# The first tokens of layer 2 summed during the last blocks of layer 1, and layer 1's last blocks in the opposite order of experts

## The chip, the core and the metric

The kernel runs on one core of a Trainium2 chip. The metric is the device time of one execution in microseconds (us), as a median of several runs. TensorE (PE) multiplies and transposes, VectorE (DVE) and ScalarE (ACT) work on elements, GpSimd (POOL) issues the gathers and scatters here, and SyncE (SP) issues nearly all other transfers.

## What is computed

A graph network of four layers on N = 2708 tokens of D = 256 features, with a dense adjacency matrix `adj`. The layer concerned is layer 1's feed-forward part and the start of layer 2's attention:

```python
def _L1_ffn_ref(x, W1, b1, Wg, bg, Wd, bd):
    H = gelu(x @ W1 + b1)                     # 256 -> 1024
    probs = softmax(H @ Wg + bg)              # 8 experts
    assign = argmax(probs)                    # one expert for each token
    for e in range(8):
        y = H @ Wd[e] + bd[e]                 # 1024 -> 256
        out = out + where(assign == e, probs[:, e:e+1] * y, 0.0)
    return out
...
x = x + L1_gnn(layernorm(x), adj, ...)
x = x + L1_ffn(layernorm(x), ...)
x = x + L2_gnn(layernorm(x), adj, ...)        # h = x @ W.T, attention over adj
```

## The kernel before

**Tiles.** Tokens lie in 22 tiles of 128 (the last has 20). `x` stays on chip with the features along a row. Layer 1 takes the tiles in three groups, 0 to 7, 8 to 15 and 16 to 21 (`GROUPS1`).

**Sending tokens to experts.** For each group, `send1` makes H (1024 wide), writes its rows to `hid` in DRAM (`keep`, two times four DMAs for each pair of tiles), finds each token's expert, and lets `route` (L385) work out each token's place in a list sorted by expert. `scatter` (L510, issued at L513 on POOL) writes (token, probability) there, to `taken`. So an expert's tokens form stretches of the list, which `blocks` (L423) cuts into blocks of 128 rows, with the expert of each block (`ei`) and the rows to be read (`ix`). The first nine blocks (`NA`, called full) are cut from the first two groups, so that they can be worked on while the third is still sent; the other fifteen (`ALWAYS`, called rest here) follow, and are taken in the order that `in_thirds` (L1066) gives. If tokens are spread more unevenly, more than fifteen are needed: `count_left` finds how many are left over, `blocks_left` loads that into a register of each engine (for block 13), and `run_rest` (L632) has a branch, `tc.If(left > 0)` in L634, behind the last block, in which up to six more run.

**A block** (class `Units`, L638) takes these steps. POOL gathers its 128 names (`fetch_names`, L657 by L527), then the 128 rows of H for them, 512 KB (`fetch_rows`, L667). SP loads the expert's matrix, 1152 KB, into one of three buffers (`weights1`, L1070, the DMA at L1077); that DMA is made only if the buffer holds another expert's matrix. PE transposes the rows (`turn`, eight of L678), ACT copies them (L679). PE multiplies, 16 matmuls in L729. DVE adds the bias (L730) and scales by the probability (L731), and POOL scatters the rows to `given` in DRAM (L513). `more` (L689) keeps names, rows and matrices fetched ahead, the matrices two blocks. `pieces` (L709) is a generator: `send1` calls `next(fill)` to put steps of the full blocks between steps of the third group.

**Order.** The program's scheduler keeps the order of the text unless `after`, `engine_after`, `in_order` or `behind` add dependencies. [...] POOL issues names, rows and scatters of all blocks in one sequence, and SP the writes of `hid`, the matrices and the loads of layer 2.

**Layer 2's front.** `turned_up` (L1428) takes two or four tiles (`FOURS`: one group of 2, then five of 4). SP loads their rows of `given` (buffer `mine`, by `load_tiles`, L56), DVE or POOL adds them to x (L1441; DVE for tiles 0 to 5, POOL for the rest), PE transposes (L1446), ACT copies (L1448), DVE makes the norm's statistics (L193). `valued` (L1452) multiplies by the layer's matrix (L267), ACT and DVE make `hh` and `sc` (L1461, L1464), `row_scores` (L1362) turns the scores. Each load waits for all scatters to `given`, and for the branch. Then the attention's long loop runs (L1540 on DVE, L1548 on PE).

Of the kernel before, what the change touches and what calls it, by code (L numbers as in the profile page):

```python
# [15 lines left out]
P = 128  # L16
N = 2708
# [49 lines left out]
def adj_ffn4(ctx: ExitStack, tc: tile.TileContext, a: dict, out: bass.AP):  # L67
# [355 lines left out]
    def blocks(pool, brief, known, NB, B, name, done=None, full=False, least=0):  # L423
# [26 lines left out]
        if done is not None:  # L450
            rest = pool.tile([P, E], F32, name="b_rest")
            v.scalar_tensor_tensor(rest, done, -float(B), cnt, op0=ALU.mult, op1=ALU.add)
            if least:
# [9 lines left out]
        bi = count[:, :NB, None]  # L463
        v.tensor_tensor(hot, bi.to_broadcast([P, NB, E]),
                        end[:, None, :].to_broadcast([P, NB, E]), ALU.is_ge)
# [3 lines left out]
        v.tensor_scalar(ei, eb[:, :, 0], float(E - 1), None, op0=ALU.min)  # L469
        v.tensor_tensor(vec[:, 0, :], nb[:, :, 0], end, ALU.subtract)  # L470
# [35 lines left out]
        return ei, ix, end[:, E - 1 :], nb[:, :, 0]  # L506
# [131 lines left out]
    class Units(Blocks):  # L638
# [3 lines left out]
        def __init__(self, pool, given, weights, hidden):  # L642
# [3 lines left out]
            self.names = pool.tile([P, MOST, 2], F32, name="names")  # L646
            g.memset(self.names, 1.0)
            self.hs = [pool.tile([P, HC * P], F32, name="hs", tag="hs", bufs=3) for _ in range(3)]
            for h in self.hs:
                g.memset(h, 0.0)  # L650
# [12 lines left out]
        def fetch_rows(self):  # L663
# [5 lines left out]
                                 bounds_check=n - 1, oob_is_err=False)  # L669
            self.got = i.ins.name  # L670
            self.rows.append((m, h))

        def turn(self, pool, h):
            hT = pool.tile([P, HC, P], F32, name="hTs", bufs=2)
# [7 lines left out]
        def begin(self, items):  # L682

            self.names_todo = list(items)
            self.todo = list(items)
            self.rows_todo = len(items)
            self.more(False)

        def more(self, weights=True):  # L689
            while self.names_todo and len(self.named) + len(self.rows) < len(self.hs) + 1:  # L690
                self.fetch_names(self.names_todo.pop(0))
            while self.rows_todo and len(self.rows) < len(self.hs):
                self.fetch_rows()
                self.rows_todo -= 1
            while weights and self.todo and len(self.ahead) < 2:
                self.fetch(self.todo.pop(0))

        def add(self, items):
            self.names_todo += items
            self.todo += items  # L700
            self.rows_todo += len(items)
            self.more()
# [6 lines left out]
        def pieces(self, pool, during=None):  # L709
# [4 lines left out]
            while self.rows:  # L714
                if len(self.rows) > 1:
                    turned.append(self.turn(pool, self.rows[1][1]))
                    yield
                w2, hT = self.ahead.pop(0), turned.pop(0)
                m, _ = self.rows.pop(0)
                self.more()  # L720
                if during is not None:
# [3 lines left out]
                y = (pool.tile([P, D], F32, name="ys", bufs=2) if self.outputs % 5 < 2 else  # L725
                     work.tile([P, D], F32, name="xn"))
                q = pools["psum"].tile([P, W], F32, name="yacc", bufs=2)[:, :D]
                for f in range(HC):
                    te.matmul(q, lhsT=hT[:, f, :], rhs=w2[:, f, :], start=(f == 0), stop=(f == HC - 1))  # L729
                v.tensor_tensor(y, q, w2[:, HC, :], ALU.add)  # L730
                i = v.tensor_scalar(y, y, m[:, 1:2], None, op0=ALU.mult)  # L731
                self.last = i.ins.name
                scatter(self.given, m[:, 0:1].bitcast(I32), y, self.given.shape[0] - 1, self.ok)
# [323 lines left out]
    ALWAYS = 15  # L1057
    with ExitStack() as l1:
# [5 lines left out]
        wbs, reads = {"held": []}, []  # L1064
# [5 lines left out]
        def weights1(b, e):  # L1070

            held = wbs["held"]
            if len(held) < 3:
                held.append([wbs["pool"].tile([P, 2048 + D], F32, name="wb", bufs=3), None])
# [47 lines left out]
        def send1(tiles, ready=None, fill=None):  # L1122
# [3 lines left out]
            names = gt.tile([P, GM, 2], F32, name="names", bufs=1)[:, :G]  # L1126
# [986 lines left out]
```

## Time and profile before

| What | us |
|---|---|
| Median of three runs (1893.95, 1893.99, 1900.85) | 1893.99 |
| The profiled execution | 1890.82 |
| Its span | 1889.1 |
| PE busy | 1816.3 (96%) |
| DVE busy | 1072.4 (57%) |
| ACT busy | 655.3 (35%) |
| POOL busy | 393.3 (21%) |
| Last matmul of layer 1's blocks ends at | 1059.8 |
| First transposes of layer 2 start at | 1071.55 |
| Attention's long loop from | 1107.15 |

All times of events are counted from the start of the span. A row of a timeline has start, length, engine, line and operation, output and inputs, how many instructions follow one another, and in brackets the idle time before it and what ended it. A row of the waits has who waited, for whom, and then the sum, the number and the longest. A releaser is inferred: of several semaphores it is the one that came last. PE's granted clock is given as a share of full speed.

### The profile page before, as it was taken

The page shows a single profiled execution, that of the slowest core. Times are in us where ns is not written, and L with a number is a line of the kernel's source. Part 1 is how long each engine was busy: PE and PEld are TensorE (multiplying, and loading weights), DVE is VectorE, ACT ScalarE, POOL GpSimd, SP SyncE. Part 2 cuts the span into 40 slices and gives each one's busy share as a digit, 9 for nine tenths or more (in the row PEclk, how much of TensorE's full clock was granted, in tenths as well). Part 3 has the DMA queues.
Part 4 walks back from the last instruction along what each step waited for, and adds up shares of the span by engine and source line. Part 5 has one row for each costly group of instructions (what it writes and reads, how often), then busy time and mean ns, then how long its engine had stood idle before and what let it go on. Part 6 is the DMA issues. An engine that isn't in the chain of part 4 may idle for free.

```text
span 1889.1 us, 25828 instructions
## 1 busy us (share of the span) xinstructions
PE 1816.3 (96%) x9453; PEld 1331.8 (70%) x9453; DVE 1072.4 (57%) x2451; ACT 655.3 (35%) x1472; POOL 393.3 (21%) x466
## 2 busy tenths in 40 slices
PE   8999999999999999999999699998899999999998
PEld 7888788888888888887788588887566633233344
DVE  8687872443343424444532365555345498888877
ACT  8777742222223203112322223223233542132232
POOL 0015354333321002303357400000000100011020
PEclk9999999999998999999999899999899999999999
DMA  8535658887763453644777440000101000012020
GB/s 272 156 100 165 227 193 295 320 313 295 277 265 125 141 152 103 173 119 121 209 235 250 159 65 9 1 1 1 45 1 35 17 1 23 23 26 37 23 37 18
DMA packets 93214, 237.52 MB, mean 126 GB/s; under 512 B 18288, under 2 KB 49048, under 8 KB 85017
## 3 DMA queue, kind: packets, MB, share of 16 engines
q1 hardware_dynamic: 71512, 189.18, 30.9%
q0 software_dynamic: 21568, 46.61, 9.0%
q8 instruction: 78, 1.28, 0.3%
q14 instruction: 56, 0.45, 0.1%
HBM read 218.39 MB, written 30.80 MB: 132 GB/s over the span
## 4 chain that ended last, share of the span: by engine, by line
PE 40%; DMA 4%; DVE 3%; issue 2%; ACT 1%; POOL 1%; POOLq 0%; SPq 0%; ACTq 0%; DVEq 0%
PE num L2014 10%; PE ps_acc L1548 9%; PE den L2022 6%; PE ps_tmp L375 4%; PE ps_acc L1757 3%; PE ps_tmp L267 2%; PE yacc L729 2%; DMA names<-taken,b_ix 1%; DMA hs<-hid,names 1%; DMA L_gnn_a_r<-in_L_gnn_a_r 1%; PE ps_acc L267 1%; DVE e L1985 1%; DMA mine<-given 1%; PE ps_acc L678 1%; PE ps_tmp L220 0%
## 5 line engine op out<-in xcount | busy, mean ns | idle before, releaser
L1985 DVE SCALAR_TENSOR_TENSOR e<-arena,G,mask 128x1024 f32<-128x1024 f32 (+1 forms) x252 | 275.0, 1149 | 34.1 <-PE den L2022 33.2
L2014 PE MATMUL num<-e,wh 128*64 128x512 f32 (+4 forms) x1056 | 214.0, 549 | 0.7 <-ACT L_gnn_W L1368 0.3
L1548 PE MATMUL ps_acc<-hh,e 128*128 128x257 f32 x882 | 199.2, 382 | 1.7 <-ACT o L1491 1.7
L1312 PE MATMUL acc<-sup,adrow 128*128 128x256 f32 x882 | 198.5, 382 | 1.5 <-DMA adrow<-in_adjT 1.5
L943 PE MATMUL acc<-msg,wt 128*128 128x256 f32 x882 | 197.6, 381 | 1.6 <-DVE wt L893 1.2
L1312 PEld LDWEIGHTS acc<-sup,adrow 128*128 128x128 f32 x882 | 165.1, 190 | 29.4 <-issue 5.5
L1548 PEld LDWEIGHTS ps_acc<-hh,e 128*128 128x128 f32 x882 | 163.8, 190 | 29.1 <-ACT o L1491 4.3
L943 PEld LDWEIGHTS acc<-msg,wt 128*128 128x128 f32 x882 | 165.1, 190 | 27.0 <-DVE wt L893 1.8
L591 PE MATMUL ps_acc<-xTs,wa 128*128 128x256 f32 (+1 forms) x768 | 169.3, 373 | 2.6 <-DVE xTs L581 2.6
L593 ACT ACTIVATE hTs<-ps_acc,wa 128x256 f32<-128x256 f32 (+1 forms) x192 | 88.7, 464 | 235.2 <-PE yacc L625 160.8
L625 PE MATMUL yacc<-wb,hTs 128*128 128x256 f32 x736 | 168.4, 380 | 0.0
L591 PEld LDWEIGHTS ps_acc<-xTs,wa 128*128 128x128 f32 x768 | 136.6, 190 | 28.6 <-DVE xTs L581 5.1
L2014 PEld LDWEIGHTS num<-e,wh 128*64 128x64 f32 (+1 forms) x1056 | 70.1, 136 | 122.7 <-issue 104.9
L625 PEld LDWEIGHTS yacc<-wb,hTs 128*128 128x128 f32 x736 | 137.2, 190 | 17.8 <-DVE ys L627 0.5
L1540 DVE SCALAR_TENSOR_TENSOR e<-Rb,G,mask 128x640 f32<-128x640 f32 (+2 forms) x110 | 85.0, 774 | 91.1 <-PE ps_acc L1548 90.4
L2022 PE MATMUL den<-e,wh 128*32 128x512 f32 (+4 forms) x1056 | 112.3, 546 | 0.0
L1277 DVE TENSOR_SCALAR mask<-adrow 128x1024 uint8<-128x1024 f32 (+1 forms) x66 | 41.7, 632 | 120.3 <-DMA adrow<-in_adjT 120.2
L221 ACT COPY xT<-ps_tmp 128x256 f32<-128x256 f32 x76 | 26.8, 366 | 198.9 <-PE ps_tmp L220 198.4
L729 PE MATMUL yacc<-wb,hTs 128*128 128x256 f32 x384 | 88.3, 384 | 0.8 <-DMA wb<-in_L_ffn_Wdp 0.8
L893 DVE SCALAR_TENSOR_TENSOR wt<-adrow,wt 128x640 f32<-128x640 f32 (+3 forms) x67 | 71.1, 1063 | 25.4 <-ACT wt L141 25.1
L2022 PEld LDWEIGHTS den<-e,wh 128*32 128x32 f32 (+1 forms) x1056 | 33.1, 109 | 73.6 <-issue 69.6
L513 POOL DMA_INDIRECT given<-ys,xs x46 | 65.8, 1431 | 81.1 <-DVE ys L628 67.9
(472 smaller groups left out, 2631.0 us busy)
## 6 DMA issues: line engine op xcount, KB each, us to landing
adhalf<-in_adjT SPq DMA_DIRECT2D x42, 677.0 KB
wb<-in_L_ffn_W2p SPq DMA_DIRECT2D x24, 1152.0 KB
wb<-in_L_ffn_Wdp SPq DMA_DIRECT2D x24, 1152.0 KB
wa<-in_L_ffn_W1b SPq DMA_DIRECT2D x24, 1028.0 KB
adrow<-in_adjT SPq DMA_DIRECT2D x42, 512.0 KB
adrow<-in_adjT SPq DMA_DIRECT2D x42, 320.0 KB
adrow<-in_adjT SPq DMA_DIRECT2D x21, 576.0 KB
adrow<-in_adjT SPq DMA_DIRECT2D x21, 448.0 KB
```

What stands on the lines that cost most here:

```text
L375: te.matmul(p[:, :w], lhsT=w1[:, c, f * P : (f + 1) * P], rhs=xnT[:, c, c0 : c0 + w], start=(c == 0), stop=(c == DC - 1))
L591: i = te.matmul(p[:, f % 2, : m * P], lhsT=w1[:, c, f * P : (f + 1) * P], rhs=xT[:, c, : m * P], start=(c == 0), stop=(c == DC - 1))
L593: s.activation(hT[:, f, : m * P], p[:, f % 2, : m * P], AF.Gelu, bias=bias[:, f : f + 1])
L625: te.matmul(q[:, k, :], lhsT=hT[:, f, k * P : (k + 1) * P], rhs=w2[:, f, :], start=(f == 0), stop=(f == HC - 1))
L729: te.matmul(q, lhsT=hT[:, f, :], rhs=w2[:, f, :], start=(f == 0), stop=(f == HC - 1))
L943: te.matmul(p[:q, n - pair[0], :], lhsT=wt[:, k : k + q], rhs=msg[:r, j, :], start=(j == 0 and n == pair[0]), stop=(j == FULL - 1 and n == ...
L1312: te.matmul(p[:q, n - pair[0], :], lhsT=ad[:, k : k + q], rhs=sup[:, jj, :], start=(jj == 0 and n == pair[0]), stop=(jj == FULL - 1 and n ...
L1540: i = v.scalar_tensor_tensor(e[:r, :w], Rb[:r, c0 : c0 + w], G[:r, j, :], mask[:r, j, c0 : c0 + w], op0=ALU.max, op1=ALU.mult)
L1548: te.matmul(p[:, : D + 1], lhsT=e[:, k : k + q], rhs=hh[:, j, :], start=(j == 0), stop=False)
L1985: v.scalar_tensor_tensor(e[:, :w], slow[:, m % 2, k, :w], G[:, j, 2 * pair + k, :], mask[:, j, c0 : c0 + w], op0=ALU.max, op1=ALU.mult)
L2014: te.matmul(num[k * DK : (k + 1) * DK, hf, :q], lhsT=wh[some, j, 2 * pair + k, :DK], rhs=e[some, :q], start=(j == 0), stop=(j == FULL), ti ...
L2022: te.matmul(den[z * Q : (z + 1) * Q, :q], lhsT=wh[some, i, 2 * pair + k, DK : DK + 1] .to_broadcast([some.stop - some.start, Q]), rhs=e[so ...
```

## The change

Each edit in words, and then the diff, cut to its core.

- The order of experts of the rest's blocks is turned round (`early` in `blocks`): from the last expert to the first. From the counts that the first group had when it was routed (`known[1][1]`, tiles 0 to 7) a number is worked out for the last block that holds a row of those tiles. If it is over nine (`AHEAD1`), or if fifteen blocks are not enough, `left` is above zero.
- The branch stands ahead of the tenth of the rest's blocks (`branch()`), behind the scatter of the ninth; in it `all_again` would do all that is left, one block at a time.
- Behind the branch SP loads tiles 0 to 7 of `given` (two loads of four tiles), with waits on the scatters made so far. DVE adds tiles 0 to 3 behind block 20 and 4 to 7 behind block 21 (numbers count full blocks first, from 0); the statistics of tiles 0 to 5 are made ahead too. The transposes stay in `turned_up`, which leaves out loads and adds of those tiles; where a group of four is mixed (6 to 9), the second half is made behind the products of the group before (`finish`). DVE adds tiles 8 to 13 now, POOL 14 to 21.
- The rest's matrices have three buffers of their own (pool `w1r`), in the memory that the gate's buffers leave free. The first three are fetched as soon as the rest's blocks are known.
- Names are fetched three ahead. `send1` lets two pieces of blocks in ahead of `route` instead of three. The last `keep` goes behind `route`'s first steps on DVE. The transposes of the first rest block lie amid the matmuls of the last full one (`late`).

```diff
@@ blocks
+        begins = end
+        if early is not None:
+            begins = pool.tile([P, E], F32, name="b_begin")
+            v.tensor_scalar(begins, end, -1.0, end[:, E - 1 :], op0=ALU.mult, op1=ALU.add)
...
+        if early is not None:
+            v.tensor_scalar(eb, eb, -1.0, float(E), op0=ALU.mult, op1=ALU.add)
...
+        rest = pool.tile([P, E], F32, name="b_rest")
+        v.scalar_tensor_tensor(rest, done, -float(B), early, op0=ALU.mult, op1=ALU.add)
...
+        v.tensor_reduce(last, begins, AX.X, ALU.max)
+        return ei, ix, end[:, E - 1 :], last
@@ class Units
+            if self.past is not None and self.places[1] == self.border - 1:
+                after(i, self.past)
...
         def begin(self, items):
+            for _ in self.hs:
+                self.fetch_names(self.names_todo.pop(0))
             self.more(False)
         def more(self, weights=True):
-            while self.names_todo and len(self.named) + len(self.rows) < len(self.hs) + 1:
-                self.fetch_names(self.names_todo.pop(0))
             while self.rows_todo and len(self.rows) < len(self.hs):
+                if not self.named:
+                    self.fetch_names(self.names_todo.pop(0))
                 self.fetch_rows()
                 self.rows_todo -= 1
+            while self.names_todo and len(self.named) < (3 if self.places[1] >= self.border else 1):
+                self.fetch_names(self.names_todo.pop(0))
             while weights and self.todo and len(self.ahead) < 2:
                 self.fetch(self.todo.pop(0))
+            if weights:
+                self.fetch_rest(2)
+        def fetch_rest(self, most):
+            while self.rest and len(self.rest_ahead) < most:
+                self.rest_ahead.append(self.weights(self.border + self.at[1], expert_of(self.rest.pop(0))))
+                self.at[1] += 1
         def add(self, items):
             self.names_todo += items
-            self.todo += items
+            self.rest += items
             self.rows_todo += len(items)
+            self.fetch_rest(3)
             self.more()
+        def all_again(self, pool, items, w2, some):
+            m = self.names[:, NA + ALWAYS, :]
+            xs, hT = self.early[0], self.hTs[1]
+            for item in items:
...
+                self.turn(pool, xs, hT)
+                self.output(pool, m, hT, w2.rearrange("p (f d) -> p f d", d=D))
@@ pieces
+                if ahead is not None and n in ahead:
+                    ahead[n]()
+                    split = len(nc.cur_bb.bb.instructions)
+                late = n == self.border - 1
-                if len(self.rows) > 1:
+                if len(self.rows) > 1 and not late:
@@ layer 1
-    ALWAYS = 15
+    ALWAYS, AHEAD1 = 15, 9
+    EARLY, prepared = GROUPS1[0], {}
@@ weights1
-            held = wbs["held"]
+            held = wbs["held" if b < NA else "rest"]
@@ send1
-                for _ in range(3):
+                for _ in range(2):
                     next(fill)
...
                 keep(*was, nc.sync)
+                engine_after(kept, mybir.EngineType.DVE, ranked)
@@ beside
-            if b == NA + 9:
+            if b == NA + AHEAD1 + 1:
                 work1.at_end = scattered["given1"][-1].name
+            if b in (NA + ALWAYS - 3, NA + ALWAYS - 2):
+                first = len(nc.cur_bb.bb.instructions)
+                for t0 in EARLY[::2][(b - NA - ALWAYS + 3) * 2 :][:2]:
+                    add_early(t0)
+                engine_after(first, mybir.EngineType.DVE, work1.last)
+            if b == NA + ALWAYS - 1:
+                for some in FOURS[:2]:
+                    prepared[some[0]] = stats(some, by_log=True)[1]
@@ layer 1, the rest's blocks
-        rest = blocks(hw, gt, known, MOST - NA, P, "B", done=full[2])
-        too_many = count_left(hw, (rest[2], ALWAYS))
+        rest = blocks(hw, gt, known, MOST - NA, P, "B", done=full[2], early=known[1][1])
+        too_many = count_left(hw, (rest[2], ALWAYS), (rest[3], AHEAD1))
         gate.close()
+        wbs["more"] = l1.enter_context(tc.tile_pool(name="w1r", reuse_waits="tile", bufs=1))
+        work1.early = [wbs["more"].tile([P, HC * P], F32, name="mine", bufs=2) for _ in range(2)]
...
+        order = in_thirds(AHEAD1) + [AHEAD1 + b for b in in_thirds(tail)]
+        def branch():
+            with tc.If(left[0] > 0):
+                work1.all_again(hc, items[AHEAD1:], wbs["rest"][2][0],
+                                slice(NA + AHEAD1, NA + ALWAYS))
+            pin(scattered["given1"][-1].name)
+            wbs["rest"][2][1] = None
+            known_rows = list(scattered["given1"])
+            for t0, o in zip(EARLY[::4], work1.early):
+                for i in load_tiles(nc, o.rearrange("p (t d) -> p t d", d=D), range(t0, t0 + 4),
+                                    given[1], t0):
...
+                    behind(i, known_rows)
+        def add_early(t0):
+            o = work1.early[t0 // 4].rearrange("p (t d) -> p t d", d=D)
+            xs = x[:, t0 : t0 + 2, :]
+            v.tensor_tensor(xs, xs, o[:, t0 % 4 : t0 % 4 + 2, :], ALU.add)
+        work1.add([items[b] for b in order])
         for _ in between:
             pass
-        for one in wbs["held"]:
-            one[1] = None
-        work1.run_rest(hc, more, left[0])
@@ turned_up
-                adder = v if t0 < FOURS[2][0] else g
+                adder = v if t0 < FOURS[4][0] else g
+                late = [t for t in tiles if t not in EARLY]
+                if late:
+                    o = gp.tile([P, 4, D], F32, name="mine", bufs=2)
+                    for i in load_tiles(nc, o, late, given[1], t0):
+                        behind(i, scattered["given1"])
...
+                        if t0 + i in EARLY:
+                            continue
                         xs = x[:q, t0 + i : t0 + i + m, :]
                         adder.tensor_tensor(xs, xs, o[:q, i : i + m, :], ALU.add)
...
+                def scale():
+                    return prepared[t0] if t0 in prepared else stats(tiles, by_log=True)[1]
...
+                def finish():
+                    had, first = last_of(fronts), len(nc.cur_bb.bb.instructions)
+                    for k in range(n - len(late), n, 2):
+                        two(k)
```

## The prediction

> **What bounds the kernel now.** I read the page's busy table first: PE is busy 1816.3 us of the 1889.1 us span (96%), so only idle or slow PE time can be won. The view by windows then shows where it lies (columns: length; busy us with instructions of PE, PEld, DVE, ACT, POOL; granted PE clock, DMA share, GB/s):
>
> ```profile
> 985.00:1060.00 75.00, 71.75 (x380) 62.59 (x378) 16.04 (x41) 17.39 (x31) 49.15 (x52) 0.98 0.69 239
> 1060.00:1107.00 47.00, 32.59 (x169) 25.43 (x169) 26.06 (x80) 19.65 (x75) 13.70 (x20) 0.85 0.31 89
> 1107.00:1321.00 214.00, 207.13 (x1011) 172.46 (x1010) 116.39 (x275) 56.34 (x214) 8.59 (x25) 1.00 0.09 11
> ```
>
> The front of layer 2 (1060 to 1107) is the hole: 14.4 us idle, clock 0.85, every other engine idle for longer. Around it PE is 96% busy, so a shift of the front's end reaches the program's end. PE's waits between 940 and 1110 name the causes:
>
> ```profile
> PE ps_tmp L1446 <- DVE x L1441: 12.2, 2, 11.7
> PE ps_acc L678 <- DMA hs<-hid,names: 6.4, 3, 4.2
> PE ps_acc L267 <- DVE hh L1464: 1.8, 1, 1.8
> PE yacc L729 <- DMA wb<-in_L_ffn_Wdp: 0.8, 1, 0.8
> ```
>
> PE's timeline at the boundary shows the wait, and matmuls of 0.49 us (2.95/6) after it where warm ones take 0.23 (3.65/16):
>
> ```profile
> 1052.66 7.14 PE L729 MATMUL yacc<-wb,hTs 128*128 128x256 f32 x32 [0.84 <-DMA wb<-in_L_ffn_Wdp]
> 1071.55 1.12 PE L1446 MATMUL ps_tmp<-ident,x 128*128 128x128 f32 x4 [11.75 <-DVE x L1441]
> 1073.49 2.95 PE L267 MATMUL ps_acc<-w_l,xT 128*128 128x258 f32 x6
> ...
> 1090.85 3.65 PE L267 MATMUL ps_acc<-w_l,xT 128*128 128x258 f32 x16
> ```
>
> POOL, SP and DVE say what the 11.75 us consist of:
>
> ```profile
> 1060.93 0.98 POOL L513 DMA_INDIRECT given<-xn,names  x1 [2.47 <-DVE xn L731]
> 1066.72 0.14 POOL L1457 MEMSET sc<- 128x8 f32 x2 [4.80 <-DMA given<-ys,names]
> 1067.21 11.14 SPq L56 DMA_DIRECT2D mine<-given  x5
> 1070.81 0.69 DVE L1441 TENSOR_TENSOR x<-x,mine 128x512 f32<-128x512 f32 x1 [10.15 <-DMA mine<-given]
> ```
>
> The last block's scatter goes out at 1060.93, the first load of the sums 6.28 us later, lands 3.6 us after that, and is added. The 6.28 are more than a scatter's landing (median 2.9 us from 1040 on, in the view of DMA issues), because the branch of L634 stands between; its rows say what it costs:
>
> ```profile
> L634 PEldq COMPARE_BRANCH  x2: 327/2100/3872, 588.7 to 1056.2; - x2
> L634 POOLq INC_SWDGE_SEM  x2: 955/1684/2413, 595.5 to 1064.1; - x2
>   PE ps_tmp L1039: 2.1, 1
> ```
>
> POOL's reset of its DMA semaphores starts at 1064.1 and takes 2.41 us; in layer 0, where PE had work on both sides, PE lost 2.1 us.
>
> [...]
>
> **The change, part by part.** Against the profiled execution, 1890.8 us (span 1889.1); the median of the runs is 3.2 us higher, 1893.99.
>
> *Sums of tiles 0 to 7 early.* In the built order PE's transposes of x still follow the last block's matmuls; only loads, adds and statistics move. After the last block PE then has 12 transposes at 0.13 (x8 take 1.04) and six tiles' products at 0.91 (3.65 for four), 7.0 us, and two more tiles' transposes, 0.5. The last scatter still goes out 1.1 us after the last matmul, lands after 2.9, the load takes 3.6, the add 0.7: 8.3 us, and I allow 0.7 for SP's issue, so tile 8 is ready at 9.0 against 7.5 of cover. Gone: 11.75 us and the cold clock, 1.75, read where a wait of similar kind stands by itself: after it 8 transposes take 1.35 and 16 matmuls 5.06 instead of 1.04 and 3.62:
>
> ```profile
> 984.79 1.35 PE L678 MATMUL ps_acc<-ident,hs 128*128 128x128 f32 x8 [4.19 <-DMA hs<-hid,names]
> 985.94 5.06 PE L729 MATMUL yacc<-wb,hTs 128*128 128x256 f32 x16
> ...
> 991.71 3.62 PE L729 MATMUL yacc<-wb,hTs 128*128 128x256 f32 x16
> ```
>
> New: 1.5. Of the 1.8 us behind DVE's hh about 1.0 goes, since POOL adds only tiles 14 to 21 (its adds take 1.27 us, DVE's 0.69); DVE holds the rest, with 26.06 us of work in the window. Sum: -11.75 -1.75 +1.5 -1.0 = -13.0 (bounds -15, with no bubble and all 1.8 gone, and -9, when DVE adds 4 us of waits to a front of 29).
>
> *The branch amid the blocks.* It moves from the end to behind block 17's scatter. PE has work on both sides: +2.1 (layer 0's row; 1 to 4, the whole 3.87 of its compare being the end). ACT's table load after it (1.28 us) lies beside 4.33 us of a block's matmuls. It isn't taken: the inputs' counts put the last block with early rows at the eighth of nine, and need exactly the fifteen blocks.
>
> *Sums' loads ahead of block 20's matrix.* On SP two loads of 512 KB stand behind the branch and ahead of the matrices of 20 to 23, and wait for POOL: 6.3 us after block 17's scatter. Blocks take 4.33 us (PE's timeline, 1017.01 to 1047.32). Counting from the last matmul of 17: scatter at 1.1, SP free at 7.4; 1.05 MB of sums and 1.18 MB of matrix at 327 GB/s (the view by windows for 985 to 1010) take 6.8[...]: 15.2. PE wants block 20 after two blocks and the bubble, 8.7 + 2.1 = 10.8. Stall 4.4[...]. Bounds: 0 if SP need only see block 17's scatter land (1.1 + 2.9 + 6.8 = 10.8); 12 if POOL must first see gathers of rows land (one took 10.7 us at 1039.22). Blocks 21 to 23 follow at 3.6 us a matrix, under 4.33. Block 22's old 0.84 is gone. Sum +5.1.
>
> *Route one piece earlier, rest's matrices in their own buffers.* The sent names go out one block (4.3 us) earlier; the gathers of the rest's rows start earlier, with names three ahead. So the waits on hs go: 4.19 + 1.68 + 0.52, and 1.75 of cold clock, 8.1. But on SP the second of the rest's own matrices waits until all names have landed, and block 3's matrix (not even loaded, its expert is the same) stands behind it. Names would be sent until about 961 and landed 7.7 us later, as before (965.3 to 973.04); with half of that still to come when PE is ready for block 3 at about 961.4, it waits 4 to 7.5 us, and 1.75 cold: 5.8 to 9.3. I take 8.1: zero net (-4 to +4, and -8 if SP is passed in time).
>
> *The rest.* Opposite expert order: 16 matrices loaded instead of 15, the last six all real; 3.6 us of DMA, costed above, where before one of two was skipped (0.07 instead of 0.33 us of issue). The new ten or so DVE operations for the expert order (0.1 to 0.3 us each) lie behind the names' landing; DVE is busy 18.25 of 45 us there. DVE's early adds (0.69 us each) are queued after block 20's and 21's scaling, behind them the next bias add, which has 3.6 us of matmuls to wait for: nothing. Ten loads of layer-2 parameters on POOL (1.3 us each) move behind a later scatter; POOL works 49.15 of 75 us: nothing, and some 3 us if they come ahead of the last scatters.
>
> Sum: -13.0 + 2.1 + 5.1 + 0 = -5.8; 1885.0 for the profiled execution, **1888.2** for the median.
>
> **The rivals.**
> A, likeliest, 0.45: as worked out, most of the gap at the end comes back as waits on SP's queue: 1881 to 1893.
> B, neither SP wait bites, 0.22: -13.0 + 2.1 - 8.1 - 0.84 = -19.8, so 1874. For it: at block 20 it is enough that SP passes the branch on the scatter alone; against it: POOL's reset held SP in layer 1 and, 5.06 us from 591.80, in layer 0, and the names took 7.7 us to land.
> C, both bite harder, 0.20: 9.3 at block 3 and 8 at block 20 give -13.0 + 2.1 + 1.2 + 8.7 = -1.0, and with DVE's 4 us +3: 1893 to 1897.
> D, slower, 0.13: from the branch on the transfers are the bound. The sums, four matrices and their rows (1.05 + 4.7 + 1.0 = 6.8 MB) at the 189 GB/s of 1010 to 1037 take 36 us. From SP's 7.4 the last lands at 43.4 and its block ends at 46.9, against 10.8 + 17.3 = 28.1 without a wait: 18.8 instead of my 5.9, and three more cold starts at 1.75: +18.1, so 1906. It makes the kernel slower by more than 0.5% below about 205 GB/s (33 us). Against it: 189 was what was asked for there; 327 was carried just before.
> That the early sums don't come early is excluded by the built order, a taken branch by the counts.
>
> **How the numbers follow.** What a measurement tells from no change is 0.5%, 9.5 us: 1884.5 to 1903.5. Faster: B and three tenths of A, 0.36. Slower: D, 0.13. Same: the rest, 0.51. The range 1872 to 1900 takes in A, B and C and leaves out D and the far side of B, under 0.2. A alone is 1881 to 1893.
>
> **What would show it.** Right: the wait of L1446's first transposes falls from 11.75 to under 2 us; block 20's matmuls wait 3 to 7 us for wb; PE has a hole of about 2 us behind block 17; block 3 waits 4 to 7 us for wb or SP, and hs waits are gone; the last block ends near 1066. Wrong: no wait at 3 or 20 (then B), PE clock under 0.9 in the last six blocks with a wait on wb at each (then D), or a front over 33 us with waits on DVE hh (then my 13.0 is too large).

## The result, and the profile after

The changed kernel takes 1900.89 us (median of 22 runs, 1896.97 to 1911.71) against 1895.70 us for the kernel before (22 runs, 1890.32 to 1902.49): a ratio of 1.0026, 95% interval 1.0015 to 1.0037, so about 5 us slower. By the bound of the prediction that is no change, but its sign is plain, and 1900.9 lies just above the predicted range.

The profiled execution has a span of 1895.8 us, 6.7 more than before. The view by windows of the changed kernel (length; busy us of PE, PEld, DVE, ACT, POOL; granted PE clock, DMA share, GB/s) shows that the hole has moved:

```profile
985.00:1060.00 75.00, 65.13 (x342) 56.54 (x341) 15.03 (x38) 16.31 (x29) 47.21 (x47) 0.95 0.67 226
1060.00:1107.00 47.00, 40.89 (x201) 33.63 (x200) 25.62 (x82) 18.74 (x67) 15.76 (x23) 0.94 0.42 132
```

PE works 8.3 us more in the stretch in which the front lay (32.59 before) and 6.6 less in the blocks ahead of it (71.75 before). PE's waits between 930 and 1115 (for whom; sum, number, longest) name what is new:

```profile
PE yacc L779 <- DMA wb<-in_L_ffn_Wdp: 12.3, 2, 6.7
PE ps_tmp L1485 <- ACT sc L1614: 2.8, 1, 2.8
PE ps_acc L708 <- PEq L1456: 2.6, 1, 2.6
PE ps_acc L708 <- DMA hs<-hid,names: 1.7, 2, 1.3
```

The 11.75 us of waiting for the first sums are gone, and so are most of the 6.4 for rows; in their place stand two waits for matrices, one at the branch and one for `sc`. PE's timeline puts them in order: block 3, the branch ahead of block 18, block 20, and the front:

```profile
970.92 8.58 PE L779 MATMUL yacc<-wb,hTs 128*128 128x256 f32 x32 [6.70 <-DMA wb<-in_L_ffn_Wdp]
...
1040.91 1.06 PE L708 MATMUL ps_acc<-ident,hs 128*128 128x128 f32 x8 [2.58 <-PEq L1456]
1041.82 5.30 PE L779 MATMUL yacc<-wb,hTs 128*128 128x256 f32 x16
...
1057.93 5.98 PE L779 MATMUL yacc<-wb,hTs 128*128 128x256 f32 x16 [5.61 <-DMA wb<-in_L_ffn_Wdp]
...
1068.95 7.07 PE L779 MATMUL yacc<-wb,hTs 128*128 128x256 f32 x32
1075.86 1.47 PE L1579 MATMUL ps_tmp<-ident,x 128*128 128x128 f32 x12
...
1082.37 0.27 PE L1485 MATMUL ps_tmp<-ident,sc 128*2 128x128 f32 x1 [2.79 <-ACT sc L1614]
...
1082.91 5.77 PE L267 MATMUL ps_acc<-w_l,xT 128*128 128x258 f32 x18
```

Layer 2's first transposes now follow the last block at once (1075.86): the early sums did what they were to do. But 16 matmuls take 5.30 us after the branch and 5.98 after the wait at 20 instead of 3.62, and the front's 18 take 5.77 after the wait for `sc`, where 18 later ones (at 1102.62) take 4.09: each of these holes cost its length and a slow start after it. PE's granted clock in the three stretches was 0.72 (1040.9 to 1047.1), 0.61 (1057.9 to 1063.9) and 0.71 (1082.9 to 1088.7), and 1.00 from 1047.8 to 1051.4 and from 1064.6 to 1068.2.

Two timelines show what stands in whose way. SP's, after block 17: the loads of the sums, held until 1046.59 (SP's waits name the landing of the scatter, 11.5 us), and behind them the matrices:

```profile
1046.59 0.94 SPq L56 DMA_DIRECT2D mine<-given  x2
1048.52 16.22 SPq L1157 DMA_DIRECT2D wb<-in_L_ffn_Wdp  x4
```

POOL's, behind the last block: the last scatter, six loads of layer 2's parameters (a seventh came ahead of it), and only then the memsets of `sc`. ACT's timeline has the activation that needs them:

```profile
1077.15 1.01 POOL L537 DMA_INDIRECT given<-xn,names  x1 [1.71 <-DVE earlier L1537]
1078.15 0.61 POOL L121 DMA_DIRECT2D L_ffn_br<-in_L_ffn_br  x1
...
1080.92 0.74 POOL L1526 DMA_DIRECT2D w_l<-in_L_gnn_WT  x1
1081.63 0.18 POOL L1610 MEMSET sc<- 128x8 f32 x2
```

```profile
1081.81 0.41 ACT L1614 ACTIVATE sc<-ps_acc,var 128x2 f32<-128x2 f32 x2 [3.75 <-POOL sc L1610]
```

The sum of the two profiles, each term a difference of starts of PE's matmuls (changed less before):

| Stretch | us |
|---|---|
| Up to block 0 (947.96 against 944.94): not explained; `r_before` and `e6_before_nobranch`, programs alike up to there, differ by 3.9 (957.87 and 961.76) | +3.0 |
| Blocks 0 to 17 (block 17: 1034.72 against 1030.00) | +1.7 |
| Branch: blocks 18 and 19 (1047.83 against 1038.66) | +4.4 |
| Block 20 waits (1057.93 against 1042.99), and its matmuls run slowly (block 21: 1064.62 against 1047.32) | +5.8 +2.4 |
| Block 22's old wait is gone | -1.0 |
| Front, end of the last block to the end of L267: 34.5 against 43.4 | -8.9 |
| Together (the front ends at 1110.57 against 1103.24, +7.3) | +7.4 |

### The profile page after: what moved, and what is told of

Read it like the earlier page. It is cut to its first block, busy times and chain, and to the rows that moved or that the text cites. A ratio compares the mean times of both kernels' runs of the same rounds, so it can differ in the third digit from the quotient of the medians.

```text
span 1895.8 us, 25846 instructions
## 1 busy us (share of the span) xinstructions
PE 1819.2 (96%) x9453; PEld 1330.8 (70%) x9453; DVE 1074.9 (57%) x2465; ACT 655.9 (35%) x1472; POOL 389.0 (21%) x462
## 5 line engine op out<-in xcount | busy, mean ns | idle before, releaser
L649 PE MATMUL yacc<-wb,hTs 128*128 128x256 f32 x736 | 168.4, 380 | 0.0
L649 PEld LDWEIGHTS yacc<-wb,hTs 128*128 128x128 f32 x736 | 137.1, 190 | 17.9 <-DVE ys L651 0.6
L779 PE MATMUL yacc<-wb,hTs 128*128 128x256 f32 x384 | 92.5, 397 | 12.3 <-DMA wb<-in_L_ffn_Wdp 12.3
L779 PEld LDWEIGHTS yacc<-wb,hTs 128*128 128x128 f32 x384 | 75.0, 200 | 23.2 <-issue 12.9
```

The costliest lines, as they stand in the source:

```text
L649: te.matmul(q[:, k, :], lhsT=hT[:, f, k * P : (k + 1) * P], rhs=w2[:, f, :], start=(f == 0), stop=(f == HC - 1))
```

## The experiments

**The theories.** Q, mine: the given-back time is a matter of order on two queues. Block 20's matrix stands behind the sums on SP, and the memsets of `sc` behind the parameters on POOL; with another order and the same transfers both waits go, and only the branch stays. V, the rival: the added 1 MB of sums and the matrices are too much for the DMA engines there, and any order waits somewhere. B, a second rival: the branch is the cause, since its `INC_SWDGE_SEM` on POOL (2.08 us from 1044.2 in the changed kernel; the prediction's reset) holds POOL and through it SP. As to block 3, S says that SP's order (the rest's second matrix ahead of block 3's) costs time, its rival that PE would wait there for rows instead.

Each group below ran on one chip, with the kernel before among its runs; ratios are to that. In the first two groups the kernel before itself took 1908.5 and 1909.9 us, in the last two 1894.4 and 1892.0, so absolute times are compared inside a group only.

### One edit at a time

`e1_params`: the parameters go behind the last of the front's memsets.

```diff
-        wr = mat(tp, "L2_ffn_Wr", E)
+        wr = tp.tile([P, DC, E], F32, name="L2_ffn_Wr", bufs=1)
...
+        def params():
...
+                if k == len(FOURS) - 1:
+                    params()
```

> The changed kernel, with the seven loads of layer-2 parameters on POOL issued behind layer 2's last clearing of sc instead of around the last scatter. Theory (waits behind other instructions on SP's and POOL's queues took the gain): the wait of 2.8 us behind the products of tiles 2 and 3 and the slow matmuls after it (1.7 us) go, so 4.5 us less than the changed kernel, 1896.4 if that is 1900.9. Rival (the transfers' volume is the bound, queues only show it): no change, within 1 us, since no byte moves before the front. A second rival: the front is bound by DVE and ACT, and the wait comes up again behind hh, 1 to 2 us gained.

Measured: 1917.17 us, 1.0038 (1.0025 to 1.0052). Its PE timeline has no wait for `sc`, and the front takes 30.1 us (1104.67 to 1134.75), where `e3_behind20` and the changed kernel, with the parameters in place, have 34.6 and 34.5. In POOL's timeline the memsets (1106.75) stand directly behind the last scatter (1105.80).

So 4.5 us of the front were due to POOL's order.

`e2_nobranch`: the branch is left out, but the sums are kept ahead of block 20's matrix.

```diff
+            if b == NA + AHEAD1 + 2:
+                after(i, work1.mine)
...
-            with tc.If(left[0] > 0):
-                work1.all_again(hc, items[AHEAD1:], wbs["rest"][2][0],
-                                slice(NA + AHEAD1, NA + ALWAYS))
```

> The changed kernel without its branch (what it would do for more uneven tokens is left out; for these inputs it does nothing), and with block 20's matrix still issued behind the loads of the early sums. Theory: PE's hole behind block 17 (2.6 us and 1.7 us of slow matmuls) goes, and SP waits for the scatter's landing alone, not for POOL's reset, so the wait of 5.6 us (8.1 with slow matmuls) for block 20's matrix falls to under 2: 9 to 12 us less, 1889 to 1892. Rival (volume): the matrices of 20 to 23 and the sums still come at some 300 GB/s, the wait at block 20 or 21 stays at 4 us or more, only the 4.3 us of the hole go: 1896.

Measured: 1920.18 us, 1.0059 (1.0043 to 1.0075). PE's timeline has no hole at the branch, but block 20 waits for longer:

```profile
1081.69 6.41 PE L779 MATMUL yacc<-wb,hTs 128*128 128x256 f32 x16 [7.76 <-DMA wb<-in_L_ffn_Wdp]
```

SP issued the sums at 1069.78, 6.0 us after block 17's scatter (1063.77), and the matrix at 1071.30, 10.4 us before it could be used. B falls as the cause of this wait: without reset and branch SP is held nearly as long (6.0 us behind the scatter, 6.7 in the changed kernel; its waits name the scatter's landing, 10.4 us), and the matrix is still behind.

`e3_behind20`: the sums' loads go behind block 20's matrix.

```diff
+            if b == NA + AHEAD1:
+                load_early()
...
+        def load_early():
```

> The changed kernel with the loads of the early sums issued on SP behind block 20's matrix instead of ahead of it; the branch stays. Theory: the matrix goes out when SP has passed the branch, about 4 us earlier and without the sums' bytes ahead: PE's wait at block 20 falls from 5.6 us to 0 to 2 and the slow matmuls go, 6 to 8 us less, 1893 to 1895. Rival (volume): the same bytes are asked for in the same stretch, the wait moves to blocks 21 and 22, within 2 us of the changed kernel. Third: SP's passing of the branch is itself what holds the matrix (its wait ends with POOL's reset), then 2 to 3 us less.

Measured: 1916.21 us, 1.0038 (1.0021 to 1.0054). Block 20 doesn't wait; block 21 does, for 3.04 us:

```profile
1081.93 3.69 PE L779 MATMUL yacc<-wb,hTs 128*128 128x256 f32 x16 [3.04 <-DMA wb<-in_L_ffn_Wdp]
```

So part of the wait moved by one block in this run, which is what V says; the next group decides whether it must.

`e4_sporder`: block 3's matrix goes ahead of the rest's second.

```diff
-            if weights:
+            if weights and not self.todo:
...
-            self.fetch_rest(3)
```

> The changed kernel with the rest's first matrices fetched only when all nine full blocks have theirs, so that no wait for the sent names stands ahead of block 3's matrix on SP. Theory: PE's wait of 6.7 us at block 3 and 1.5 us of slow matmuls go, but the rows of the first rest blocks still come when the names have landed, so some 4 us come back as a wait for hs at block 9: 2 to 5 us less, 1896 to 1899. Rival: the rows are late by all of it, the wait only changes its place, within 1 us. Against both: up to 8 us less if the names that were fetched ahead let the rows come in time.

Measured: 1915.45 us, 1.0035 (1.0022 to 1.0048). The wait for block 3's matrix is gone, but PE stands idle for 6.81 us in the transposes ahead of its matmuls, which the trace puts down to nothing that it can name ("issue", at 984.59).

The changed kernel's own ratio in the next group is 1.0055: each of e1, e3 and e4 is 0.17 to 0.20% below it, less than the width of any of the four intervals. Alone, they decide by their traces, not by their times.

### All three together, and both kernels again

`r_before` and `r_after` are the two kernels as they are, for their traces on this chip.

> The kernel before, unchanged, for its trace beside those of this chip: four experiments ran where the kernel before itself took 1908.5 us, and their traces show PE and ACT idle in layer 1's blocks with no releaser (issue, remote), which the first traces do not. If the chip does that, this trace shows it too, some 5 to 10 us in blocks 9 to 12; if the changed kernels do it, it does not.

> The changed kernel, unchanged, as the reference for the others of this call: 1.0026 times the kernel before, 1.001 to 1.004, if the chip doesn't matter to the ratio; 1.006 to 1.008 if what was seen in the four experiments (none of them under 1.0035, while each took away a wait of 4 to 8 us) lies in the chip.

Measured: 1910.41 us (one run) and 1920.90 us, 1.0055 (1.0036 to 1.0074). Here the change costs twice as much as in its first measurement. Both traces have idle stretches in the blocks from 3 on that are not in the first profiles, such as one of 10.07 us ahead of a block's transposes in the kernel before (at 987.47, put down to ACT's copy of `hTs`). What they are wasn't found. The waits at block 20 (4.79) and for `sc` (2.78) are there as before.

`e5_all`: the edits of e1, e3 and e4 together.

> The changed kernel with three edits at once: parameters behind the front's clearing of sc, the early sums' loads behind block 20's matrix, the rest's matrices fetched when the full blocks have theirs. Theory (waits behind other instructions on the two queues): 4.5 + 5 + 2 to 5 us less than the changed kernel on the same chip, so 12 to 15, some 0.6 to 0.8%. Rival (volume of transfers): under 6 us less. Rival (the edits only shift one wait into the next): within 3 us of it.

Measured: 1905.44 us, 0.9982 (0.9970 to 0.9993), 15 us under `r_after`. In PE's timeline no wait for a matrix is left from block 18 on, and one hole stays, at the branch:

```profile
1057.97 1.94 PE L708 MATMUL ps_acc<-ident,hs 128*128 128x128 f32 x8 [3.35 <-DMA given<-xn,names]
```

The same sums and the same matrices are moved, without a wait, so V falls in its strict form, that any order waits somewhere. But the branch's hole and the slow start behind it give the transfers some 6 us here (3.35, and 1.94 and 5.65 for transposes and matmuls that otherwise take 1.04 and 3.62). In `e3_behind20`, with the same order on SP and no slow start behind the hole (2.85, then 3.62 for 16 matmuls), block 21 waited for 3.04 us; e7 and e12 show what is left without the branch.

`e6_before_nobranch`: the kernel before without its branch.

```diff
-        work1.run_rest(hc, more, left[0])
+        pin(scattered["given1"][-1].name)
```

> The kernel before without the branch at the end of layer 1 (what it would do for more uneven tokens is left out). It measures how much of the hole of 11.75 us is the branch's: the last scatter lands after 2.9 us instead of 6.3 until SP goes on, so the hole falls to 8.4 us and the time by 3.4 us (0.18%) if the branch only adds POOL's reset; by 5 us or more if SP could also pass earlier; by nothing if the load waits for the parameters' loads on POOL.

Measured: 1905.70 us, 0.9976 (0.9963 to 0.9990), 0.24% under the kernel before, 4.6 us. The wait for the first sums is 7.04 us, with the branch (`r_before`) 10.66:

```profile
1087.92 1.12 PE L1446 MATMUL ps_tmp<-ident,x 128*128 128x128 f32 x4 [7.04 <-DVE x L1441]
```

So the branch stood for 3.6 us of the hole that the change was made to close. (The whole front is only 1.4 us shorter in this trace, 40.8 against 42.2, since a slow start followed a later wait for DVE's `hh`: 12 matmuls took 4.57 us after 2.14 of waiting, 2.88 after 1.59 in `r_before`.)

### One edit taken back from the three

`e7_all_nobranch`: e5 without the branch.

> The version with all three edits (parameters behind, sums' loads behind block 20's matrix, rest's matrices fetched later), and without the branch (what it would do for more uneven tokens is left out). It prices the branch amid the blocks by itself, now that no load waits behind it that PE wants soon: 2.6 us of hole and 1.7 to 2 us of slow matmuls, so 4 to 5 us (0.2 to 0.25%) less than the version with three edits, about 0.9960 times the kernel before. If the branch costs only what was forecast, 2.1 us: 0.9971. If SP's way through it still holds block 20's matrix: 0.994.

Measured: 1892.06 us, 0.9989 (0.9975 to 1.0003). Not faster than e10 below, which has the branch: PE now comes to block 21 without a hole, and that block's matrix, which SP issues behind the sums, at 1051.41, is late in turn:

```profile
1060.08 6.33 PE L778 MATMUL yacc<-wb,hTs 128*128 128x256 f32 x16 [6.11 <-DMA wb<-in_L_ffn_Wdp]
```

So this run couldn't price the branch, since another wait came in its place; with the same order on SP and with the branch (e5), PE had a hole of 3.35 us and the slow start ahead of block 18, and no wait at block 21.

`e8_no_behind20`, `e9_no_params` and `e10_no_sporder`: e5 without the edit of e3, of e1 and of e4.

> The version with three edits less one: the early sums' loads stand ahead of block 20's matrix again, as in the changed kernel. Queue order as cause: PE waits 4 to 6 us for block 20 again, with 2 to 3 us of slow matmuls, 5 to 8 us (0.3 to 0.4%) over the version with three edits (0.9982), so 1.001 to 1.002. Volume as cause: no difference, 0.998.

> The version with three edits less one: the seven loads of parameters stand ahead of the front's clearing of sc on POOL again. The front has its wait of 2.8 us behind sc and 1.7 us of slow matmuls again: 4.5 us (0.24%) over the version with three edits, so 1.0005. If DVE and ACT bound the front: within 1 us, 0.9985.

> The version with three edits less one: the rest's first three matrices are fetched as soon as its blocks are known, ahead of block 3's, as in the changed kernel. The wait at block 3 comes back, but other waits in blocks 3 to 12 (rows, ACT) shrink by it: 2 to 5 us (0.1 to 0.25%) over the version with three edits, so 0.9995 to 1.0007. If the rows bound blocks 3 to 12 in any case: 0.998 to 0.9985.

Measured:

| Kernel | us | Ratio (95%) |
|---|---|---|
| e8_no_behind20 | 1897.29 | 1.0021 (1.0011 to 1.0030) |
| e9_no_params | 1896.67 | 1.0007 (0.9992 to 1.0023) |
| e10_no_sporder | 1890.06 | 0.9979 (0.9969 to 0.9989) |

PE's timelines: in e8 block 20's wait is back, in e9 that for `sc`; e10 has neither, but the wait at block 3 (6.33 us, at 969.73) and the branch's hole. One fence for each, in this order:

```profile
1059.65 5.59 PE L778 MATMUL yacc<-wb,hTs 128*128 128x256 f32 x16 [6.21 <-DMA wb<-in_L_ffn_Wdp]
```

```profile
1077.92 0.27 PE L1489 MATMUL ps_tmp<-ident,sc 128*2 128x128 f32 x1 [2.77 <-ACT sc L1618]
...
1078.47 4.09 PE L267 MATMUL ps_acc<-w_l,xT 128*128 128x258 f32 x18
```

```profile
1043.33 1.94 PE L708 MATMUL ps_acc<-ident,hs 128*128 128x128 f32 x8 [3.59 <-DMA given<-xn,names]
```

Against e10, e8 is 7.2 us slower and e9 6.6 (8.0 and 5.3 by the ratios); both also differ in SP's order at block 3. The traces agree for e8, whose stretch from block 17 to the last block is 6.9 us longer than e10's. In e9 the front takes 32.8 us against 30.0: the wait is there, but no slow start followed it. That order is worth nothing: e5 with it (0.9982) and e10 without it (0.9979) cannot be told apart. In e8 and e9 the waits for rows are 8.0 us and more (e9 has one of 9.47), and from block 0 to block 13 the kernels before, changed, e8, e9 and e10 take 66.9, 68.6, 70.1, 71.8 and 70.8 us. S falls: the wait only changes its place.

### The branch and the early sums by themselves

`e11_behind23`: e10 with the sums' loads behind the last matrix, and their adds and statistics later. `e12_behind23_nobranch`: the same without the branch.

```diff
-            if b == NA + AHEAD1:
+            if b == NA + ALWAYS - 3:
                 load_early()
...
-            if b in (NA + ALWAYS - 3, NA + ALWAYS - 2):
+            if b == NA + ALWAYS - 1:
```

> The version with parameters behind, and the early sums' loads on SP behind the last block's matrix (block 23's) instead of block 20's; all four adds stand behind block 22's scaling, statistics behind the last block's. Queue order as cause: no matrix is behind the sums' loads any more, so no wait for a matrix in blocks 18 to 23; the branch's hole stays; 0.9970 to 0.9980 times the kernel before, as the version with the loads behind block 20's (0.9979). If the bytes themselves bound the last blocks: a wait of 3 us or more at block 22 or 23 and 1.000.

> The same without the branch (what it would do for more uneven tokens is left out). If the branch amid the blocks costs its hole and the slow matmuls after it, 4 to 5 us: 0.995 to 0.9958. If the matrices of the last six blocks can't come faster than with the hole (six in a row to be loaded), a wait for one comes in the hole's place and the time stays: 0.9970 to 0.9980.

Measured: 1894.56 us, 1.0010 (0.9997 to 1.0023), and 1888.32 us, 0.9985 (0.9975 to 0.9995). Both fronts are spoilt by my edit (4.29 us of waiting for ACT's `xT`, in both), so neither is the best version. But here the branch has no other wait to trade places with, and the difference is its price: 0.0025, 4.7 us by the ratios (6.2 by the medians; each ratio is known to about 0.001, 2 us). From the start of block 17 to the last block's end e11 takes 34.4 us and e12 28.8. In e11's PE timeline the hole and the slow start are these:

```profile
1049.07 1.94 PE L708 MATMUL ps_acc<-ident,hs 128*128 128x128 f32 x8 [3.46 <-DMA given<-xn,names]
1050.80 4.43 PE L779 MATMUL yacc<-wb,hTs 128*128 128x256 f32 x16
```

3.46 + 0.9 + 0.8 = 5.2 us (8 transposes otherwise take 1.04, 16 matmuls 3.62). In e12 the same stretch has no hole and no wait, with the sums behind all matrices; but there they come late for the front, which takes 38.2 us against e10's 30.0. So for a kernel without the branch V isn't refuted: e7 waits at block 21, e12 pays in the front (for late sums, and for the late statistics of this edit), and an order between the two wasn't tried.

The same stretch of all runs, from the start of block 17 to the last block's end (us, from PE's timelines), shows how the two prices hide one another:

| Sums' loads on SP | With the branch | Without |
|---|---|---|
| Behind all matrices, or none early | 34.4 (e11), 34.5 (e13) | 28.8 (e12) |
| Behind block 20's matrix | 34.4 (e10), 34.9 (e9), 35.2 (e5), 35.3 (e3), 36.3 (e14) | 37.7 (e7) |
| Ahead of block 20's matrix | 41.3 (changed), 40.3 to 41.8 (r_after, e1, e4, e8) | 39.9 (e2) |

The branch alone costs 5.7 us, the sums behind block 20's matrix alone 8.9, and both together 5.7 to 7.6, hardly more than the branch. With the sums ahead of that matrix, leaving out the branch gains hardly anything.

`e13_no_early`: the change with e1's edit and no early sums; the branch stays amid the blocks.

```diff
-    EARLY, prepared = GROUPS1[0], {}
+    EARLY, prepared = range(0), {}
```

> The version with parameters behind and without the early sums: all 22 tiles are loaded and added behind the last block, the branch and all else stay as in the changed kernel. The front's hole is back, without the branch's part: scatter's landing, load and add, about 8 us, and 1.75 of slow matmuls, less the 1.5 us of waits behind tile 8; block 20's matrix has no loads ahead of it, so its wait is under 3 us. Against the version with the loads behind block 20's (0.9979) 8 us more: 1.002. If the early sums gain little because DVE and ACT bound the front: 0.999.

Measured: 1893.93 us, 1.0006 (0.9996 to 1.0016). The first sums are waited for 7.09 us, and the front takes 36.8 us, against 30.0 in e10:

```profile
1081.47 1.11 PE L1581 MATMUL ps_tmp<-ident,x 128*128 128x128 f32 x4 [7.09 <-DVE x L1576]
```

The old hole of 11.75 is 4.7 us shorter with the branch moved, and amid the blocks there is a new one of 3.65 us with a slow start of 1.7; the early sums take the rest, 6.8 us in the trace and, e10 against e13 by their ratios, 0.27% or 5 us in the times.

`e14_route3`: e10 with three pieces of blocks ahead of `route` again, as before the change.

```diff
-                for _ in range(2):
+                for _ in range(3):
```

> The version with parameters behind and the loads behind block 20's matrix, and with three pieces of blocks ahead of the sending of names instead of two, as in the kernel before. If the earlier sending only moved the waits of blocks 3 to 9: within 0.0007 of 0.9979. If it gained what was forecast of it, some 4 us: 1.000. If it cost the 1.7 us by which the changed kernel is later at block 12 in the first traces: 0.997.

Measured: 1887.95 us, 0.9974 (0.9966 to 0.9983): 4 us faster than the kernel before in its group, by ratio 10 under the changed kernel, and not to be told from e10. Of the waits over 2 us in the blocks PE's timeline (of an execution at the upper end of its runs) keeps one for rows in place of block 3's, and the branch's:

```profile
977.40 1.09 PE L708 MATMUL ps_acc<-ident,hs 128*128 128x128 f32 x4 [7.51 <-DMA hs<-hid,names]
...
1045.65 1.06 PE L708 MATMUL ps_acc<-ident,hs 128*128 128x128 f32 x8 [4.10 <-DMA given<-xn,names]
```

Sending the names one piece earlier gains nothing that can be measured, as in S's rival.

## Why the prediction was wrong

Forecast was -5.8 us, measured about +5. The mechanisms of rival A, the likeliest, are all there; two terms of its sum were too small and one was left at nothing.

**The front, -13.0: right in itself.** With the parameters out of the way it takes 30.0 (e10) and 30.1 us (e1) against 43.4, so -13.4. The last scatter went out 1.1 us after the last matmul (1077.15 against 1076.02) and the next sums' loads 2.5 us later, about as worked out.

**The parameters on POOL, "nothing": the first step that failed.** I set them against POOL's busy share, saw room, and asked only what happens if they come ahead of the last scatters. They came behind the last scatter, and ahead of the memset of `sc`, for which ACT waits and then PE. The row of L1457 stood in the prediction's own excerpt. Six issues of some 0.6 us (1078.15 to 1081.63; the prediction had ten of 1.3) became a wait of 2.8 and a slow start of 1.7: the missing 4.5 us of the front (34.5 against 30.1 in e1). In e9 only the wait came, and the front lost 2.8.

**The branch, 2.1: too small.** The hole was 2.58 us, within the bounds (1 to 4), but I gave it no slow start; with 16 matmuls at 5.30 instead of 3.62 it cost 4.4, and about 5 by e11 and e12. I had read that the branch stood in the 11.75 us at the end, but not priced it there: 3.6 us of the hole in e6's trace, 4.6 in its times (1.9 to 7.1 by its interval). The sum took the whole hole off and put back 2.1, where moving the branch is worth about nothing.

**Block 20, 5.9: right in kind, too small.** (5.9 is the wait of 4.4 and 1.5 of slow matmuls.) SP was free 8.2 us after block 17's last matmul (7.4 in the prediction). The number was nearly right and its reason wrong: I had SP wait for POOL's reset, 6.3 us behind the scatter, and took 2.9 for the scatter's landing alone. At the end of layer 1 the hole was shorter without the branch (7.04 us in e6, 10.66 in `r_before`). Amid the blocks the branch made no such difference to SP: the sums' loads went out 6.0 (e2) and 6.8 us (e7) behind block 17's scatter without a branch, 6.7 with it, and in e2 SP's waits name the scatter's landing. From there I let the sums and the matrix have all 327 GB/s to themselves, 7.8 us, of which 1 was an estimate of mine for issue and landing that no trace gave; it took 11.3 (1046.59 to 1057.93). The windows of the changed kernel for that stretch show why:

```profile
1046.60:1058.00 11.40, 5.79 (x36) 5.02 (x34) 1.55 (x4) 2.15 (x4) 5.29 (x6) 0.90 0.92 339
```

The rate was as assumed, but 339 GB/s for 11.4 us are 3.9 MB, and the sums and the matrix only 2.23: rows, parameters and the next matrix shared it. Hence a wait of 5.6 in place of 4.4, though PE came later, and 2.4 of slow start in place of 1.5, an estimate of mine for which no trace stood. Full DMA engines alone didn't make PE wait here: in e10 they carry 364 GB/s between 1047 and 1058 (busy share 0.98) and PE is never idle. There SP issues block 20's matrix at 1044.01, ahead of the sums (1047.69), and PE has had the branch's hole of 3.59 us:

```profile
1047.00:1058.00 11.00, 11.00 (x61) 9.75 (x60) 1.61 (x4) 2.15 (x4) 5.27 (x6) 1.00 0.98 364
```

That a matrix behind the sums' loads comes late was only my assumption when I forecast. The runs agree with it: block 20 waits 5.61 us (the changed kernel), 4.45 (e4) and 6.21 (e8) for the matrix behind the sums, and not at all with it ahead of them (e3, e5, e10). What happens between SP's issue and the landing, no run separates.

**Blocks 0 to 17, zero (-4 to +4): right within its bounds,** +1.7. The wait at block 3 (6.70) was as forecast, and e4, e8, e9 and e14 show that it stands for waits on rows.

Together: -13.0 + 2.1 + 5.1 became -13.4 + 4.5 (`sc`) + 4.4 (branch) + 7.2 (block 20, less the old wait at 22) + 1.7 = +4.4, about what was measured (the 3.0 us ahead of block 0 are left out). Of the 10.2 us between that and the forecast, `sc` is 4.5, the branch 2.3, block 20 2.1 and the blocks up to 17 are 1.7, less 0.4 at the front. Slow starts are 4.3 of it (1.7 at the branch, 0.9 more at 20 and 1.7 at `sc`).

## What to carry to other kernels

When an instruction is moved among those that one engine issues, look for the next instruction behind it whose result somebody waits for, not for the queue's busy share: here loads of 0.6 us each ahead of a 0.2 us memset, and early sums ahead of the next matrix, gave back most of what the closed hole had brought, and two edits of order turned a kernel 0.26% slower into one 0.2% faster. Give a new hole in PE's work a slow start as the upper end of its price (at the branch it was nothing in e9 and 2.9 us in e5), and before a branch is moved find what it costs where it stands: 3.6 us of the hole that was to go were the branch's (e6 against `r_before`).

## What the runs showed of the hardware

- The branch, whose body isn't run, cost about 5 us amid PE's work (e11 against e12: 4.7 by the ratios, 5.7 in the traces), though in the changed kernel its branch instructions on the other engines take 45 to 56 ns each. PE's row ends at 1040.6, 2.2 us after block 17's matmuls (1038.34), and PE works again at 1040.91. POOL's `INC_SWDGE_SEM` starts later, at 1044.2. It isn't shown to hold SP either: the sums' loads went out 6.0 (e2) and 6.8 us (e7) behind block 17's scatter without it, 6.7 with it. What PE waits for in the hole stays open. The view of DMAs of the changed kernel has two packets of the queue q8, which it calls instruction, between 1038 and 1042; no run separates whether PE waits for them. The rows of the branch's line in the changed kernel:

```profile
L1456 PEldq COMPARE_BRANCH  x1: 5552/5552/5552, 1035.0 to 1035.0; - x1
L1456 POOLq INC_SWDGE_SEM  x1: 2078/2078/2078, 1044.2 to 1044.2; - x1
```

- The length of a hole didn't decide alone whether a slow start followed. At the branch, 16 matmuls took 5.30 us after holes of 2.44 (e8), 2.58 (the changed kernel) and 4.10 (e14), but 3.62 after 2.25 (e1), 2.85 (e3) and 2.98 (e9). The wait for `sc` is the same in the changed kernel (2.79) and in e9 (2.77), and the 18 matmuls after it take 5.77 and 4.09. What else decides isn't shown. The shortest hole at the branch with a slow start after it was 2.36 us, in `r_after`, with 4.82 for 16 matmuls:

```profile
1070.33 1.59 PE L708 MATMUL ps_acc<-ident,hs 128*128 128x128 f32 x8 [2.36 <-PEq L1456]
1071.71 4.82 PE L779 MATMUL yacc<-wb,hTs 128*128 128x256 f32 x16
```

- The same two kernels differ by 0.26% on one occasion and by 0.55% on another, with other idle stretches in the blocks. That stays open, as does a branch placed where PE waits for rows anyway, which wasn't tried.
